# The third pass of a vision-state-space and attention kernel: square root and reciprocal in place of a power on GpSimd, one bias addition moved from VectorE to GpSimd, new planned durations

## The chip, the cores and the metric

The kernel runs on one core of a Trainium2 chip. The metric is the device time of one execution in microseconds (us), given as the median of several runs. A profile is one further execution with the hardware profiler on; it has its own time and its own span, from the first to the last recorded instruction. The engines are called TensorE (PE, and PEld for its weight loads), VectorE (DVE), ScalarE (ACT), GpSimd (POOL) and SyncE (SP), whose queue issues nearly all DMAs.

## The reference

The input x is 8 images of 64 x 64 positions with 96 channels. Two layers are computed.

Layer 0 normalises x in groups of three channels, projects it to 2 x 192 channels, runs a 3 x 3 depthwise convolution and then a selective scan in four directions over the 4096 positions of each image. Its end is what matters here: the sum y of the scans is standardised over its 192 channels, scaled and shifted, gated by silu(z), projected back to 96 channels and added to x.

```
mu = jnp.mean(y, axis=-1, keepdims=True)
var = jnp.mean(jnp.square(y - mu), axis=-1, keepdims=True)
y = (y - mu) * jax.lax.rsqrt(var + 1e-05) * ln_gamma + ln_beta
y = y * jax.nn.silu(z)
out = jnp.einsum('bhwd,cd->bhwc', y, out_proj_w)
```

Layer 1 is attention without a softmax over the tokens of an image, followed by a feed-forward part in quantised numbers (products in fp8, sums rounded to 16 bits). Each of the two stands behind a standardisation over the 96 channels, `(v - m) / sqrt(s + 1e-5)`, and is added to its input:

```
t = t + attn(_ln_t(t))
t = t + ffn(_ln_t(t))
```

Without a softmax, attention needs only the 97 x 97 Gram matrix of the standardised tokens of an image. So an image's tokens must all be standardised before the first of them can go on.

## The kernel before

There are three passes: projections and convolution; the scan; and everything behind the scan. The change lies in the third, `pass3`. It works on units of 512 tokens, held as 128 partitions x 4 blocks: 8 images x 8 units, 64 units in all.

Each unit goes through a load (five DMAs: the two halves y and yo of the scan's sum, two parts of the gate zs, and x as xr) and two generators.

- `first_part` (line 979): GpSimd adds y and yo; `standardize` on y; TensorE transposes y in two steps, ScalarE evicts each (gt) and GpSimd multiplies it by zs; TensorE projects; VectorE adds xr and so makes t; `standardize` on t, into ln; TensorE adds ln to the image's Gram matrix (pg) and transposes it, and ScalarE evicts that (lnT).
- `attention` (line 1031), once per image when its eight Gram contributions are in, makes a matrix weff from the Gram matrix by four small products.
- `second_part` (line 1058): TensorE multiplies lnT by weff, VectorE adds to t; `standardize` on t, into lf; transpose and cast to fp8 (xq, VectorE); three products with the first weights (ph), evicted to f16 by ScalarE twice and VectorE once (h); VectorE adds the first bias and takes the maximum with zero, three times; GpSimd casts to fp8 (hq); TensorE makes the second product (mm); ScalarE evicts it as f16 (y16, shown by the profile as `y<-mm`); VectorE adds the second bias b2q to it (`y<-y,b2q`); GpSimd adds it to t; SyncE stores t.

`standardize` (line 947) runs three times per unit, 192 times in all. VectorE makes statistics and aggregates of the four blocks; GpSimd adds 1e-5 to the four variances of each partition and raises them to the power -1/2 (the constant tile `mhalf`); VectorE multiplies mean and deviation; ScalarE applies scale and bias to the four blocks. The profile calls the small tile mvy, mvt or mvf by what it standardises: y, t, or t again for the feed-forward part.

The order of the instructions on each engine is written at build time by a planner, `weave` (line 142). A generator yields, ahead of each step, the engine's name, a duration that the planner assumes, and, if it differs from 0.3, a delay until the result can be used; a fourth value is a pool of buffers that the step takes from. The planner simulates five engines with these durations and always issues the step that could begin first, with ties broken by rank. Up to five first parts, five second parts and one load are open at a time, and a first part ranks twelve units ahead. What comes out is a fixed order: `InOrder` (line 82) makes every instruction on TensorE, VectorE, ScalarE and GpSimd, and every DMA that SyncE issues in the pass, follow the one issued before it on that engine. It records all of them at line 91, so the profile shows line 91 for nearly everything and groups are told apart by tile names. On the chip the durations play no part any more: an engine whose next instruction isn't ready waits, with everything behind it.

The delay of 20 behind the last GpSimd step is such a planned number. It puts the store of a unit later in SyncE's queue, where a store that waits would hold up the loads behind it.

Of the kernel before, what the change touches and what calls it, by code (L numbers as in the profile page):

```python
# [33 lines left out]
F32 = mybir.dt.float32  # L34
# [3 lines left out]
AF = mybir.ActivationFunctionType  # L38
ALU = mybir.AluOpType
# [3 lines left out]
P = 128  # L43
NB, HH, WW, C = 8, 64, 64, 96
# [823 lines left out]
def pass3(ctx, tc, g, ident, mhalf, engines, y_d, z_d, out):  # L868
    nc = tc.nc
    pe, dve, act, pool = engines  # L870
    CA = C + 1
    sp = InOrder(tc, nc.sync)
    wp = ctx.enter_context(tc.tile_pool(name="p3w", bufs=1))
# [4 lines left out]
    NU = GRP // P  # L878
# [5 lines left out]
    gates = ctx.enter_context(tc.tile_pool(name="p3gates", bufs=3))  # L884
    held = ctx.enter_context(tc.tile_pool(name="p3held", bufs=HELD))
    banks = {"tr": 3, "mm": 2, "ph": 2}
    slots = {name: Slots(count) for name, count in {**banks, "loaded": LOADED, "held": HELD, "gates": 3}.items()}
    pools = {name: ctx.enter_context(tc.tile_pool(name=f"p3{name}", bufs=count, space=PSUM)) for name, count in banks.items()}
    ps_one = ctx.enter_context(tc.tile_pool(name="p3ps", bufs=1, space=PSUM))

# [28 lines left out]
    def load_quantized(shape, src, name):  # L922
        raw = one.tile([P, *shape[1:]], F32, name=f"{name}_raw", tag="raw")
        if shape[0] < P:
            nc.vector.memset(raw[shape[0] : P], 0.0)
        nc.sync.dma_start(raw[0 : shape[0]], src)
        q = wp.tile([P, *shape[1:]], F8, name=name)
        nc.vector.tensor_copy(q, raw, saturate=False)
        return q
# [6 lines left out]
    b2q = load_quantized([P, C], g["b2"].unsqueeze(0).to_broadcast([P, C]), "b2q")  # L936
# [4 lines left out]
    def take(name, shape):  # L941
        return pools[name].tile(shape, F32, name=name), slots[name].taken

    def tokens(src, q):
        return src[q * GRP : (q + 1) * GRP].rearrange("(n p) c -> p n c", p=P)

    def standardize(src, dst, name, cost):

        yield "dve", 4 * cost
        st = each.tile([P, NU, 6], F32, name=f"st{name}")  # L950
        mv = each.tile([P, NU, 2], F32, name=f"mv{name}")
        for i in range(NU):
            dve.bn_stats(st[:, i, :], src[:, i, :])
        for i in range(NU):
            dve.bn_aggr(mv[:, i, :], st[:, i, :])
        yield "pool", 1.3
        pool.tensor_scalar(mv[:, :, 1], mv[:, :, 1], 1e-5, None, ALU.add)
        pool.tensor_tensor(mv[:, :, 1], mv[:, :, 1], mhalf[:, 0:NU], ALU.pow)
        yield "dve", 0.15
        dve.scalar_tensor_tensor(mv[:, :, 0], mv[:, :, 0], -1.0, mv[:, :, 1], ALU.mult, ALU.mult)  # L960
        yield "act", 4 * cost
        for i in range(NU):
            act.activation(dst[:, i, 0 : src.shape[2]], src[:, i, :], AF.Identity, bias=mv[:, i, 0:1], scale=mv[:, i, 1:2])
# [15 lines left out]
    def first_part(b, q):  # L979
        yield "load", b, q  # L980
        y, yo, zs, xr, of_loads = loads[b, q]
        yield "pool", 1.8, 0.3, slots["held"]
        t, lnT = held.tile([P, NU, C], F32, name="t"), held.tile([P, GRP], F32, name="lnT")
        holds[b, q] = t, lnT, slots["held"].taken
        pool.tensor_add(y, y, yo)
        yield from standardize(y, y, "y", 0.45)
        for i, ch in enumerate((slice(0, P), slice(DI - P, DI))):
            yield "pe", 0.6, 0.3, slots["tr"]
            pt, slot = take("tr", [P, GRP])
            for n in range(NU):  # L990
                pe.transpose(pt[:, n * P : (n + 1) * P], y[:, n, ch], ident)
            end = yield ("act", 0.65) if i else ("act", 0.65, 0.3, slots["gates"])
            if i == 0:
                gt, of_gt = gates.tile([P, 2, GRP], F32, name="gt"), slots["gates"].taken
            act.activation(gt[:, i, :], pt, AF.Identity, bias=gb[:, i, 1:2], scale=gb[:, i, 0:1])
            slots["tr"].release(slot, end)
            yield "pool", 1.3
            pool.tensor_mul(gt[:, i, :], gt[:, i, :], zs[:, i, :])
        end = yield "pe", 3.8, 0.3, slots["mm"]
        slots["gates"].release(of_gt, end)  # L1000
        po, slot = take("mm", [P, NU, C])
        for i in range(NU):
            blk = slice(i * P, (i + 1) * P)
            pe.matmul(po[:, i, :], gt[:, 0, blk], w_out0, start=True, stop=False)
            pe.matmul(po[:, i, :], gt[:, 1, blk], w_out1, start=False, stop=True)
        end = yield "dve", 0.55, 0.0
        dve.tensor_add(t, po, xr)
        slots["mm"].release(slot, end)
        slots["loaded"].release(of_loads, end)
        ln = lns[(b * UNITS + q) % OPEN]  # L1010
        yield from standardize(t, ln, "t", 0.35)
        if b > 0:
            yield "gram", b - 1
        end = yield "pe", 1.6
        if b not in grams:
            grams[b] = ps_one.tile([P, CA], F32, name="pg")
        counts["gram", b] = counts.get(("gram", b), 0) + 1
        for i in range(NU):
            first, last = counts["gram", b] == 1 and i == 0, counts["gram", b] == UNITS and i == NU - 1
            pe.matmul(grams[b], ln[:, i, :], ln[:, i, 0:CA], start=first, stop=last)  # L1020
        if counts["gram", b] == UNITS:
            done["grams", b] = end
        yield "pe", 0.7, 0.3, slots["tr"]
        pl, slot = take("tr", [P, GRP])
        for i in range(NU):
            pe.transpose(pl[:, i * P : (i + 1) * P], ln[:, i, :], ident)
        end = yield "act", 0.6
        act.copy(lnT, pl)
        slots["tr"].release(slot, end)
# [28 lines left out]
    def second_part(b, q):  # L1058
        yield "weff", b
        t, lnT, of_hold = holds[b, q]  # L1060
        end = yield "pe", 1.3, 0.3, slots["mm"]
        pa, slot = take("mm", [P, NU, C])
        for i in range(NU):
            blk = slice(i * P, (i + 1) * P)
            pe.matmul(pa[:, i, :], lnT[:, blk], weffs[b], start=True, stop=True)
        end = yield "dve", 0.55, 0.0
        dve.tensor_add(t, t, pa)
        slots["mm"].release(slot, end)
        lf = lfs[(b * UNITS + q) % OPEN]
        yield from standardize(t, lf, "f", 0.35)  # L1070

        yield "pe", 0.7, 0.3, slots["tr"]
        pf, slot = take("tr", [P, GRP])
        for i in range(NU):
            pe.transpose(pf[:, i * P : (i + 1) * P], lf[:, i, :], ident)
        end = yield "dve", 0.7
        xq = each.tile([P, GRP], F8, name="xq")
        dve.tensor_copy(xq, pf, saturate=False)
        slots["tr"].release(slot, end)
        h1 = each.tile([P, NHC, GRP], F16, name="h1")  # L1080
        for hc in range(NHC):
            yield "pe", 0.4, 0.3, slots["ph"]
            ph, slot = take("ph", [P, GRP])
            pe.matmul(ph, w1q[:, hc * P : (hc + 1) * P], xq, start=True, stop=True)
            end = yield ("act" if hc < 2 else "dve"), 0.6
            (act.copy if hc < 2 else dve.tensor_copy)(h1[:, hc, :], ph)
            slots["ph"].release(slot, end)
        yield "dve", 1.2
        for hc in range(NHC):
            dve.tensor_scalar(h1[:, hc, :], h1[:, hc, :], b1q[:, hc : hc + 1], 0.0, ALU.add, ALU.max)  # L1090
        yield "pool", 1.5
        hq = each.tile([P, NHC, GRP], F8, name="hq")
        pool.tensor_copy(hq, h1, saturate=False)
        yield "pe", 1.0, 0.3, slots["mm"]
        po, slot = take("mm", [P, NU, C])
        for i in range(NU):
            for hc in range(NHC):
                pe.matmul(po[:, i, :], hq[:, hc, i * P : (i + 1) * P], w2q[:, hc, :], start=hc == 0, stop=hc == NHC - 1)
        end = yield "act", 0.5
        y16 = each.tile([P, NU, C], F16, name="y16")  # L1100
        act.copy(y16, po)
        slots["mm"].release(slot, end)
        yield "dve", 0.6
        dve.tensor_add(y16, y16, b2q.unsqueeze(1).to_broadcast([P, NU, C]))

        yield "pool", 0.95, 20.0
        pool.tensor_add(t, t, y16)
        end = yield "sp", 0.7, 4.0
        sp.dma_start(tokens(out[b], q), t)
        slots["held"].release(of_hold, end)  # L1110
# [53 lines left out]
```

## Time and profile before

| | |
|---|---|
| median of 3 runs | 10,178.76 us (10,177.76 to 10,182.01) |
| the profiled execution's own time | 10,170.3 us |
| its span | 10,168.5 us |
| mean granted TensorE clock | 0.906 |
| busy over the whole span | TensorE 74%, VectorE 94%, ScalarE 90%, GpSimd 90% |
| third pass, from its first load to the last instruction | 9,328 to 10,169 us |
| busy in the third pass | TensorE 605.9 us, VectorE 635.8, ScalarE 523.2, GpSimd 672.6 |

Busy shares over the span say little on the third pass, since the scan takes most of the time and loads the engines otherwise. A row of a table of stages gives the stretch, its length, the busy time of each engine with its number of instructions, the granted TensorE clock, the mean busy share of the DMA engines and what they moved. A row of a group gives engine and operation, output and inputs by name, sizes and number; behind the first bar the busy time in us and the mean of one in ns, behind the second the idle time of the engine ahead of these instructions and what ended it. A row of the timeline gives start and duration in us, then the group, and in brackets the idle time ahead of it. A row of the waits gives who waited for whom: total us, times, longest.

### The profile page before, as it was taken

The numbers are of one execution on the slowest core, as the hardware profiler recorded it, in microseconds if no ns is written. First come the engines' busy times: TensorE is split into PE (matmuls) and PEld (weight loads), VectorE is DVE, ScalarE is ACT, GpSimd is POOL, SyncE is SP. The second block draws the span as 40 slices with busy tenths as digits, with TensorE's granted clock in tenths as the row PEclk, the third lists the DMA queues.
The fourth block names the chain that finished last, engine by engine and source line by source line (L and its number), as shares of the span: only waits on it lengthen the run. The fifth ranks groups of instructions, "written<-read, shape, count | busy, mean of one in ns | idle before, by whom it ended". The sixth has DMA issues, their size and how long they took to land.

```text
span 10168.5 us, 152388 instructions
## 1 busy us (share of the span) xinstructions
PE 7540.2 (74%) x52384; PEld 6239.7 (61%) x52384; DVE 9577.5 (94%) x6896; ACT 9175.2 (90%) x20499; POOL 9189.8 (90%) x3231
## 2 busy tenths in 40 slices
PE   7767777777777777777777777777777777776777
PEld 3336666665666666665666666666666666665665
DVE  7979999999999999999999999999999999997887
ACT  5669999999999999999999999999999999996665
POOL 1549999999999999999999999999999999997886
PEclk8889999989998999989989989899999999898887
DMA  5766776689976766799866666899666668997542
GB/s 164 236 213 219 228 232 220 228 209 208 208 221 212 227 219 214 226 205 202 224 209 223 221 212 224 209 207 208 218 215 224 217 214 222 206 204 191 156 140 72
DMA packets 932228, 2111.66 MB, mean 208 GB/s; under 512 B 274603, under 2 KB 422860, under 8 KB 929922
## 3 DMA queue, kind: packets, MB, share of 16 engines
q1 hardware_dynamic: 928650, 2100.57, 72.8%
q8 instruction: 419, 6.86, 0.3%
q14 instruction: 351, 2.88, 0.1%
q0 software_dynamic: 432, 0.94, 0.0%
q10 hardware_dynamic: 2376, 0.40, 0.0%
HBM read 1925.98 MB, written 175.66 MB: 207 GB/s over the span
## 4 chain that ended last, share of the span: by engine, by line
ACT 29%; DVE 28%; issue 16%; POOL 12%; PE 11%; DMA 3%; SPq 1%; DVEq 0%; ACTq 0%; POOLq 0%
DVE h L91 20%; ACT x L91 11%; ACT da L91 11%; POOL c L91 7%; PE acc L91 6%; DVE wide L91 5%; ACT L91 2%; PE wide L91 2%; ACT y L91 1%; POOL xg L91 1%; PE px L91 1%; ACT delta L91 1%; PE pa L91 1%; DMA xd_d<-xd 1%; DVE u L91 1%
## 5 line engine op out<-in xcount | busy, mean ns | idle before, releaser
L91 POOL TENSOR_TENSOR c<-c,h 128x2048 f32<-128x2048 f32 x1536 | 6957.3, 4553 | 292.5 <-issue 135.5
L91 DVE TENSOR_TENSOR_SCAN h<-da,carry,wide 128x1024 f32<-128x1024 f32 x2304 | 5267.8, 2331 | 133.6 <-PE wide L91 34.3
L91 ACT ACTIVATE x<-duT,bT 128x128 f32<-128x128 f32 (+1 forms) x13312 | 3994.9, 371 | 2.0
L91 PE MATMUL acc<-ident,c 128*128 128x128 f32 x24576 | 3429.8, 297 | 588.5 <-POOL c L91 581.1
L91 ACT ACTIVATE da<-delta,a_neg 128x1024 f32<-128x1024 f32 x3072 | 3520.6, 1147 | 290.4 <-DVE h L91 278.7
L91 PEld LDWEIGHTS acc<-ident,c 128*128 128x128 f32 x24576 | 3111.6, 154 | 1028.5 <-POOL c L91 918.8
L91 PE MATMUL wide<-ident,x 128*128 128x128 f32 x10752 | 1566.1, 291 | 636.5 <-DVE h L91 570.2
L91 PEld LDWEIGHTS wide<-ident,x 128*128 128x128 f32 x10752 | 1314.3, 150 | 831.0 <-ACT x L91 376.7
L91 DVE TENSOR_TENSOR_SCAN h<-da,wide 128x1024 f32<-128x1024 f32 x768 | 1712.4, 2271 | 43.9 <-PE wide L91 10.6
L91 DVE TENSOR_TENSOR wide<-du,wide 128x1024 f32<-128x1024 f32 x1280 | 1543.0, 1207 | 41.3 <-PE wide L91 40.9
L91 PE MATMUL wide<-xb,sel 96*128 96x512 bf16 x2560 | 819.8, 404 | 687.7 <-DVE h L91 671.0
L91 POOL TENSOR_TENSOR xg<-duT,bT 128x512 f32<-128x512 f32 (+1 forms) x640 | 892.4, 1409 | 27.5 <-PE wide L91 10.9
L91 PEld LDWEIGHTS <-sel 96*128 96x128 bf16 x2560 | 232.3, 102 | 867.2 <-DVE h L91 615.2
L91 PE MATMUL wide<-ident,xg 128*128 128x128 f32 x3584 | 481.1, 278 | 118.3 <-DVE h L91 116.3
L91 PEld LDWEIGHTS wide<-ident,xg 128*128 128x128 f32 x3584 | 409.6, 143 | 148.6 <-issue 110.6
L91 ACT ACT_TABLE_LOAD x385 | 494.0, 1283 | 6.8
L91 POOL TENSOR_TENSOR du<-delta,u 128x1024 f32<-128x1024 f32 x192 | 456.9, 2380 | 8.2 <-ACT delta L91 8.2
L91 DVE SCALAR_TENSOR_TENSOR u<-xpad,conv_w,u 128x4096 f32<-128x4096 f32 x96 | 452.0, 4708 | 1.9
L91 PE MATMUL px<-u,w_xp 128*128 128x512 f32 x512 | 250.2, 628 | 56.5 <-ACT u L91 41.8
L91 ACT COPY y<-acc 128x1024 f32<-128x1024 f32 x192 | 192.7, 1004 | 82.1 <-PE acc L91 81.8
L91 POOL TENSOR_TENSOR bq<-bq,bs 128x512 f32<-128x512 f32 (+1 forms) x48 | 117.7, 2453 | 162.7 <-ACT bs L91 116.3
L91 PE MATMUL wide<-ident,du 128*128 128x128 f32 x1536 | 206.9, 278 | 67.6 <-DVE h L91 34.3
(141 smaller groups left out, 6149.3 us busy)
## 6 DMA issues: line engine op xcount, KB each, us to landing
c<-xd_d SPq DMA_DIRECT2D x1024, 1024.0 KB
c<-xd_d SPq DMA_DIRECT2D x1024, 512.0 KB
u<-u_d SPq DMA_DIRECT2D x127, 512.0 KB
xdt<-dt_d SPq DMA_DIRECT2D x1146, 36.0 KB
xb<-b_d SPq DMA_DIRECT2D x382, 96.0 KB
u<-u_d SPq DMA_DIRECT2D x128, 256.0 KB
zs<-z_d SPq DMA_DIRECT2D x128, 256.0 KB
y_d<-y SPq DMA_DIRECT2D x24, 1024.0 KB
```

Source lines behind the costliest of these rows:

```text
L91: ins = getattr(self.engine, op)(*args, **kwargs).ins
```

## The change

The third pass gets a constant tile `eps` of 1e-5. In `standardize` the two GpSimd instructions go. ScalarE takes the square root of variance + eps instead (one instruction for the four variances), and VectorE makes the reciprocal in a further instruction, ahead of the product that was there. In `second_part` the addition of the second bias goes from VectorE to GpSimd, directly ahead of GpSimd's addition to t. The remaining edits are durations that the planner assumes: for the statistics and normalisations, the gate's evictions, the first bias, and the joined GpSimd step at the end.

```diff
+    eps = wp.tile([P, 1], F32, name="eps")
+    nc.vector.memset(eps, 1e-5)
...
     def standardize(src, dst, name, cost):
-        yield "dve", 4 * cost
+        yield "dve", 4 * (cost - 0.05)
...
-        yield "pool", 1.3
-        pool.tensor_scalar(mv[:, :, 1], mv[:, :, 1], 1e-5, None, ALU.add)
-        pool.tensor_tensor(mv[:, :, 1], mv[:, :, 1], mhalf[:, 0:NU], ALU.pow)
-        yield "dve", 0.15
+        yield "act", 0.25
+        act.activation(mv[:, :, 1], mv[:, :, 1], AF.Sqrt, bias=eps)
+        yield "dve", 0.4
+        dve.reciprocal(mv[:, :, 1], mv[:, :, 1])
         dve.scalar_tensor_tensor(mv[:, :, 0], mv[:, :, 0], -1.0, mv[:, :, 1], ALU.mult, ALU.mult)
         yield "act", 4 * cost
...
-        yield from standardize(y, y, "y", 0.45)
+        yield from standardize(y, y, "y", 0.54)
...
-            end = yield ("act", 0.65) if i else ("act", 0.65, 0.3, slots["gates"])
+            end = yield ("act", 0.77) if i else ("act", 0.77, 0.3, slots["gates"])
...
-        yield from standardize(t, ln, "t", 0.35)
+        yield from standardize(t, ln, "t", 0.46)
...
-        yield from standardize(t, lf, "f", 0.35)
+        yield from standardize(t, lf, "f", 0.46)
...
-        yield "dve", 1.2
+        yield "dve", 1.5
         for hc in range(NHC):
             dve.tensor_scalar(h1[:, hc, :], h1[:, hc, :], b1q[:, hc : hc + 1], 0.0, ALU.add, ALU.max)
...
-        yield "dve", 0.6
-        dve.tensor_add(y16, y16, b2q.unsqueeze(1).to_broadcast([P, NU, C]))
-        yield "pool", 0.95, 20.0
+        yield "pool", 2.2, 20.0
+        pool.tensor_add(y16, y16, b2q.unsqueeze(1).to_broadcast([P, NU, C]))
         pool.tensor_add(t, t, y16)
```

## The prediction

> **What bounds the kernel now.** Everything the change touches lies in the third pass, so I read the busy time by stage first: start-up; first parts alone (7 additions of the two scan halves); first and second parts mixed (52 such additions, 47 casts of the hidden layer); drain.
>
> ```profile
> core 0: us, PE busy (x) PEld busy (x) DVE busy (x) ACT busy (x) POOL busy (x), PEclk, DMA share, GB/s
> 9328.00:9374.00 46.00, 18.47 (x74) 14.61 (x74) 17.64 (x70) 13.68 (x27) 24.37 (x37) 0.53 0.86 249
> 9374.00:9434.00 60.00, 43.04 (x250) 39.40 (x250) 39.45 (x134) 36.57 (x78) 47.30 (x51) 0.77 0.58 177
> 9434.00:10035.00 601.00, 458.28 (x3245) 394.81 (x3246) 496.00 (x1807) 410.68 (x909) 530.50 (x557) 0.87 0.48 142
> 10035.00:10169.00 134.00, 86.10 (x529) 63.44 (x528) 82.69 (x295) 62.23 (x141) 70.48 (x77) 0.68 0.10 26
> ```
>
> The pass takes 841 of 10,168.5 us; a gain can come from nowhere else. In its main stage GpSimd is the fullest engine (530.5/601 = 88%), VectorE next (83%), ScalarE has 190 us free. The groups of this stretch say what fills GpSimd:
>
> ```profile
> L91 POOL TENSOR_TENSOR gt<-gt,zs 128x512 f32<-128x512 f32 x128 | 163.8, 1287 | 18.2 <-ACT gt L91 17.6 <-PE tr L91 0.4
> ...
> L91 POOL TENSOR_TENSOR mvt<-mvt,mhalf 128x4 f32<-128x4 f32 x64 | 67.5, 1055 | 5.3
> L91 POOL TENSOR_TENSOR mvf<-mvf,mhalf 128x4 f32<-128x4 f32 x64 | 67.4, 1053 | 5.3
> L91 POOL TENSOR_TENSOR mvy<-mvy,mhalf 128x4 f32<-128x4 f32 x64 | 66.5, 1040 | 5.3
> L91 POOL TENSOR_TENSOR t<-t,y 128x384 f32<-128x384 f32 x64 | 58.9, 921 | 29.0 <-DVE y L91 24.4 <-DVE mvf L91 2.7 <-DVE mvt L91 0.9
> ...
> L91 DVE SCALAR_TENSOR_TENSOR mvt<-mvt 128x4 f32<-128x4 f32 x64 | 51.8, 810 | 22.4 <-POOL mvt L91 21.7
> ...
> L91 DVE SCALAR_TENSOR_TENSOR mvy<-mvy 128x4 f32<-128x4 f32 x64 | 49.2, 770 | 39.2 <-POOL mvy L91 39.2
> ...
> L91 DVE TENSOR_TENSOR y<-y,b2q 128x384 f16<-128x384 f16 x64 | 43.7, 683 | 26.7 <-ACT y L91 26.7
> ...
> L91 POOL TENSOR_SCALAR mvt<-mvt 128x4 f32<-128x4 f32 x64 | 16.5, 258 | 34.2 <-DVE mvt L91 33.5 <-DVE mvy L91 0.3
> ```
>
> Four numbers to the power -1/2 take as long as 384 additions. And VectorE's product of the same four numbers takes 0.74 us on average (141.3 us over 192, mvf's 40.3 included), though its shortest took 0.126. The timeline of the second stage shows why:
>
> ```profile
> 9394.08 1.04 POOL L91 TENSOR_TENSOR mvy<-mvy,mhalf 128x4 f32<-128x4 f32 x1
> 9395.09 1.81 POOL L91 TENSOR_TENSOR y<-y,yo 128x768 f32<-128x768 f32 x1
> 9395.16 1.77 DVE L91 SCALAR_TENSOR_TENSOR mvy<-mvy 128x4 f32<-128x4 f32 x1 [2.56 <-POOL mvy L91]
> ...
> 9397.02 1.87 ACT L91 ACTIVATE y<-y,mvy 128x192 f32<-128x192 f32 x4 [2.83 <-DVE mvy L91]
> ```
>
> The power ends, GpSimd goes straight to its next addition, and VectorE's product, released at the same moment, ends with that addition. ScalarE waits for both. Here this closes a loop of 8.53 us per unit: two gate products (2.49), add and power (1.3), blocked product (1.8), normalisation (1.9), transpose and eviction (1.1). Who waited, in the main stage:
>
> ```profile
> ACT lf L91 <- DVE mvf L91: 53.6, 33, 4.5
> ACT ln L91 <- DVE mvt L91: 39.0, 27, 4.5
> ACT y L91 <- DVE mvy L91: 37.3, 21, 4.5
> ```
>
> **What the Trainium skill says.** "SBUF — State Buffer", section "Who interferes with whom": a VectorE instruction with two SBUF inputs, and casts, copies and tensor_scalar in two-port modes, are shut out while a GpSimd instruction that reads SBUF runs. The trace agrees (0.126 us free, 1.77 behind the addition). "ScalarE: Activation LUTs", section "Table sets: the hidden batching unit": copy and identity are in every set, so the square root's set serves the whole pass. The built order confirms it: one more table load than before, ahead of the first square root, none after; 1.28 us by the trace's 494.0/385.
>
> **The change part by part** (main stage: 153 standardisations, about 46 bias additions).
>
> 1. GpSimd loses 153 adds and powers: 160.4 us of powers (all instructions that read the -1/2 constants in this stage) + 153 x 0.249 = 198.5 us.
> 2. GpSimd gains 46 bias additions, f16 plus fp8, 384 elements. Not in this trace on GpSimd. Below: 0.83 us, the 2.6 cycles per element of "GPSIMD Engine Reference", section "3.1 Elementwise — side-by-side cycle accounting", an estimate; the 0.921 row is close. Above: the third-way-split subtractions of the first pass, mean 2.45 us for 512 elements, so 1.84. I take 1.1: 51 us. GpSimd: 530.5 - 198.5 + 51 = 383 (417 at the upper end, still not the fullest).
> 3. ScalarE gains 153 square roots of four numbers. Its copy of two numbers takes 0.178 us; the ScalarE page (section "What ACT_TABLE_LOAD costs") gives 280 ns + 0.833 per element with a pointer bias, an estimate of 0.283. I take 0.28: 43 us, 410.7 to 454. Its 190 free us hide this; without that cover it costs the 43.
> 4. VectorE loses 46 x 0.683 = 31 us and gains 153 reciprocals. No row; the shortest four-number product (0.126) is the floor, a reciprocal shut out as those products are (0.74) the ceiling. I take 0.16, as a one-input instruction on strided numbers: 24 us.
> 5. The products and bias-and-ReLU steps are shut out less, as GpSimd falls from 88% to about 70% full and no longer starts an operation at the product's release. Product: 0.155 free + 0.7 x 0.65 (half a mean GpSimd operation) = 0.6 for 0.74, 21 us. ReLU: three take 0.86 us where they run free in the timeline, 0.29 each, so 141 x (0.549 - 0.29) = 36 us lost today, a quarter less: 9. VectorE: 496 - 31 + 24 - 30 = 459.
> 6. New waits. The square root stands on ScalarE's queue until VectorE's aggregates are done; behind it are normalisations, evictions and hidden-layer casts of other units, for which TensorE's banks wait. The reciprocal holds VectorE until ScalarE is done; behind it are the casts to fp8 and the ReLU, for which TensorE and GpSimd's cast wait. These replace the same two hand-offs through GpSimd. The bias addition no longer heads VectorE's queue (26.7 us idle before it).
> 7. The plan's costs change only the order. In the built order the first second part follows 12 first parts instead of 11, and 12 second parts run alone at the end as before; every queue up to this pass keeps its order. DMAs are the same ones in slightly another order; at 48% DMA share I cost that at nothing, and at 5 us if loads come late.
>
> Main stage: the fullest engine becomes VectorE (459; ScalarE 454, TensorE 458 with modelled ends). GpSimd reached 88% of the stage; with three engines level I take 85%: 459/0.85 = 540, gain 61. Second stage: the loop opens, ScalarE's work per first part is 1.87 + 1.55 + 1.55 + 0.57 + 0.56 = 6.1 us; with hand-offs 7.1 for 8.5, 7 units: gain 10. Start-up, bound by loads (86% DMA share): 0. Drain, a chain of latencies: power and blocked product save about 0.8 us per link, the slower addition gives back 0.5: gain 3. Sum 74 us. The profiled execution took 10,170.3 us (span and 1.8 around it), 8.5 under the median, so 10,170.3 - 74 + 8.5 = 10,105.
>
> **The rivals.**
> - Stronger: the engines were held mostly by blocked products. Main stage at 92%: 459/0.92 = 499, gain 102; second stage at ScalarE's 6.1, gain 17; drain 13. 10,047. For: 130 us of ScalarE waiting in the lines above. Against: nothing here runs at 92%.
> - Weaker: the wait moves to square roots heading ScalarE's queue. Main stage at 80%: 574, gain 27, others 5: 10,147. For: ScalarE in program order is now on both sides of each standardisation.
> - No change: these waits eat all 74. 10,179.
> - Slower: the reciprocal is shut out by GpSimd as well. A pair of reciprocal and product at 1.5 us: VectorE 496 - 31 - 153 x 0.74 + 153 x 1.5 = 581; at 90% full 646, 45 lost: 10,224. It decides from about 1.2 us per pair, where VectorE's sum reaches today's 530. Against: one input, and the skill's section doesn't name it.
> - That each square root reloads tables is excluded by the built order.
>
> **How the numbers follow.** Likeliest 0.58 (own range 10,075 to 10,135), stronger 0.17, weaker 0.16, no change 0.05, slower 0.04. A measurement tells from no change about 0.2%, 20 us. The weaker case lies partly inside: faster 0.58 + 0.17 + 0.12 = 0.87; same 0.09; slower 0.04. The range 10,040 to 10,160 leaves out the last two cases, a tail of the stronger one and a little of the weaker.
>
> **What would show it.** Right: powers gone, GpSimd near 70% of a main stage of about 540 us, products at 0.6 us or less, reciprocals near 0.16, bias additions near 1.1, the second stage's period near 7 us, one table load. Wrong: reciprocals or products near 0.7 and VectorE above 90%; ScalarE idle ahead of square roots for over 100 us; a drain longer than 140 us.

## The result, and the profile after

The changed kernel takes 10,116.26 us (median of 4 runs, 10,114.86 to 10,131.87) against 10,178.26 before (median of 4): a ratio of 0.9941 (95% interval 0.9928 to 0.9953), 62 us faster. The forecast was 10,105, 74 us faster. The direction came out as forecast and the size near it. Of the steps behind them the prices and the opened loop of the second stage held; three steps of the sum did not (part 5, the rule for the main stage, part 7).

The profiled execution happens to be the longest of the four. The difference lies ahead of the change: its third pass began at 9,346.7 us, that of the kernel before at 9,328.1, though both issue the same instructions until there. Such scatter of the first two passes goes through all profiled executions of this study (9,328 to 9,347 us). So beside each median I give the third pass alone, from its first load of `yo` to the last instruction of the profiled execution: 840.4 us before, 783.4 after, 57 less. It is one execution each, so a few us of it may be chance.

The busy time by stage after, with the same four stages as in the prediction:

```profile
core 0: us, PE busy (x) PEld busy (x) DVE busy (x) ACT busy (x) POOL busy (x), PEclk, DMA share, GB/s
9347.00:9393.00 46.00, 18.94 (x93) 15.88 (x94) 16.85 (x80) 18.75 (x40) 20.81 (x28) 0.60 0.88 254
9393.00:9435.00 42.00, 33.06 (x232) 29.73 (x232) 31.27 (x146) 36.59 (x87) 26.75 (x20) 0.92 0.78 240
9435.00:10003.00 568.00, 442.88 (x3225) 386.86 (x3226) 482.07 (x1913) 439.69 (x1067) 374.07 (x298) 0.87 0.50 150
10003.00:10130.00 127.00, 87.41 (x549) 65.18 (x547) 78.69 (x297) 63.82 (x154) 59.96 (x55) 0.67 0.10 27
```

The main stage ends here with the last normalisation of y. Cut in the same way, the kernel before has 607 us of main stage and 128 of drain:

```profile
9434.00:10041.00 607.00, 461.43 (x3261) 396.40 (x3262) 501.85 (x1831) 415.88 (x921) 535.06 (x562) 0.86 0.47 141
```

So the gain is 18 us in the second stage (60 to 42, for the same 7 additions), 39 in the main stage, 1 in the drain. GpSimd's share of the main stage falls from 88% to 66%.

The groups after, over the third pass, that answer to those of the prediction:

```profile
L91 POOL TENSOR_TENSOR gt<-gt,zs 128x512 f32<-128x512 f32 x128 | 161.8, 1275 | 132.1 <-ACT gt L91 111.9 <-DMA zs<-z_d 15.1 <-PE tr L91 3.4
...
L91 POOL TENSOR_TENSOR t<-t,y 128x384 f32<-128x384 f32 x64 | 58.4, 912 | 5.0
...
L91 POOL TENSOR_TENSOR y<-y,b2q 128x384 f16<-128x384 f16 x64 | 56.0, 875 | 52.1 <-ACT y L91 52.0
...
L91 DVE SCALAR_TENSOR_TENSOR mvt<-mvt 128x4 f32<-128x4 f32 x64 | 46.6, 729 | 2.2
...
L91 DVE SCALAR_TENSOR_TENSOR mvy<-mvy 128x4 f32<-128x4 f32 x64 | 41.2, 643 | 2.2
...
L91 ACT ACTIVATE mvt<-mvt,eps 128x4 f32<-128x4 f32 x64 | 19.1, 298 | 15.4 <-DVE mvt L91 14.9 <-DVE mvy L91 0.3
...
L91 DVE RECIPROCAL mvt<-mvt 128x4 f32<-128x4 f32 x64 | 10.8, 168 | 10.1 <-ACT mvt L91 9.9
```

The square root takes 0.298 us, the reciprocal 0.168, the bias addition on GpSimd 0.875. The product of mean and deviation is still long: with mvf's 38.9 us, 126.7 over 192, 0.66 us. The timeline shows both sides of that, shortly before the second stage begins:

```profile
9384.53 0.18 DVE L91 RECIPROCAL mvy<-mvy 128x4 f32<-128x4 f32 x1 [3.33 <-ACT mvy L91]
9384.75 0.26 DVE L91 SCALAR_TENSOR_TENSOR mvy<-mvy 128x4 f32<-128x4 f32 x1
...
9391.54 1.81 POOL L91 TENSOR_TENSOR y<-y,yo 128x768 f32<-128x768 f32 x1
...
9391.73 1.65 DVE L91 SCALAR_TENSOR_TENSOR mvy<-mvy 128x4 f32<-128x4 f32 x1
```

The first product runs nearly free. The second meets GpSimd's addition and ends with it, as before the change. In the second stage before, 13 of the 14 products met a GpSimd addition or product from its start, since GpSimd began it at the product's release; their mean there fell from 1.42 us to 0.82. With that the loop opened: 42/7 = 6.0 us per unit for 8.5. In the main stage nearly as much is held up as before (0.70 us per product before, 0.67 after).

The waits in the main stage after, total us, times and longest:

```profile
ACT ln L91 <- DVE mvt L91: 30.9, 21, 3.8
...
ACT lf L91 <- DVE mvf L91: 20.7, 14, 3.4
...
ACT mvt L91 <- DVE mvt L91: 11.7, 9, 3.9
ACT mvf L91 <- DVE mvf L91: 11.6, 11, 2.5
ACT y L91 <- DVE mvy L91: 11.3, 10, 2.1
...
ACT mvy L91 <- DVE mvy L91: 9.8, 6, 4.5
```

In the main stage ScalarE waited 130 us for VectorE's products; it now waits 63 for them and 33 for the aggregates, ahead of the square roots.

### The profile page after: what moved, and what is told of

Its sections match the earlier page's. It is cut to its first block, busy times and chain, and to the rows that moved or that the text cites. A ratio compares the mean times of both kernels' runs of the same rounds, so it can differ in the third digit from the quotient of the medians.

```text
span 10130.1 us, 152413 instructions
## 1 busy us (share of the span) xinstructions
PE 7527.0 (74%) x52384; PEld 6235.5 (62%) x52384; DVE 9551.4 (94%) x7025; ACT 9186.9 (91%) x20692; POOL 8990.2 (89%) x2911
## 4 chain that ended last, share of the span: by engine, by line
DVE 30%; ACT 29%; issue 15%; PE 13%; POOL 9%; DMA 3%; SPq 1%; DVEq 0%; ACTq 0%; POOLq 0%
DVE h L91 20%; ACT x L91 11%; ACT da L91 10%; POOL c L91 7%; PE acc L91 6%; DVE wide L91 5%; PE wide L91 3%; ACT L91 2%; ACT y L91 1%; POOL xg L91 1%; PE px L91 1%; PE pa L91 1%; ACT delta L91 1%; DMA xd_d<-xd 1%; DVE u L91 1%
## 5 line engine op out<-in xcount | busy, mean ns | idle before, releaser
L91 POOL TENSOR_TENSOR gt<-gt,zs 128x512 f32<-128x512 f32 x128 | 161.8, 1275 | 132.1 <-ACT gt L91 111.9
```

Source lines behind the costliest of these rows:

```text
L91: ins = getattr(self.engine, op)(*args, **kwargs).ins
```

## The experiments

Every experiment edits only the third pass. Differences to the changed kernel are given as medians, then as third pass. The kernel before took between 10,164 and 10,195 us in its 34 runs of one session, and each third pass is one execution; so a few us between two kernels are not told from none.

| kernel | median us | ratio to before, 95% interval | third pass us |
|---|---|---|---|
| before | 10,178 to 10,181 | | 840.4 |
| changed | 10,116.3 | 0.9941 (0.9928 to 0.9953) | 783.4 |
| power_only | 10,118.0 | 0.9939 (0.9927 to 0.9952) | 779.2 |
| bias_only | 10,201.4 | 1.0022 (1.0015 to 1.0029) | 862.6 |
| durations_only | 10,164.1 | 0.9985 (0.9978 to 0.9992) | 824.1 |
| old_durations | 10,135.6 | 0.9957 (0.9940 to 0.9973) | 798.1 |
| more_scalar | 10,122.8 | 0.9942 (0.9926 to 0.9959) | 783.8 |
| more_vector | 10,114.6 | 0.9938 (0.9923 to 0.9952) | 779.7 |
| more_gpsimd | 10,145.5 | 0.9968 (0.9956 to 0.9980) | 801.5 |
| open_four | 10,154.2 | 0.9975 (0.9964 to 0.9985) | 816.1 |
| open_six | 10,098.9 | 0.9918 (0.9904 to 0.9933) | 764.4 |
| product_on_gpsimd | 10,094.5 | 0.9915 (0.9901 to 0.9928) | 754.4 |
| product_gpsimd_bias_vector | 10,091.0 | 0.9910 (0.9895 to 0.9925) | 747.2 |
| product_bias_six | 10,087.9 | 0.9905 (0.9888 to 0.9921) | 744.8 |

**The parts of the change, one by one.** First the changed kernel with the bias addition back on VectorE:

```diff
-        yield "pool", 2.2, 20.0
-        pool.tensor_add(y16, y16, b2q.unsqueeze(1).to_broadcast([P, NU, C]))
+        yield "dve", 0.6
+        dve.tensor_add(y16, y16, b2q.unsqueeze(1).to_broadcast([P, NU, C]))
+        yield "pool", 0.95, 20.0
```

> The changed kernel with the second bias put back on VectorE; the power is still replaced and the new planned durations stay. Theory 1 (the fullest engine of the main stage sets its length): VectorE gets back about 48 x 0.68 = 33 us in the main stage, 482 + 33 = 515 at 85% full is 605 us, as long as before the change; only the second stage's 18 us stay. So about 20 us faster than before (10,158), and the bias move is worth about 40. Theory 2 (the power's trip through GpSimd was the whole matter): the bias move is worth nothing, 55 to 65 us faster than before.

61 us faster than before: as fast as the whole change. Theory 1 falls on its own number. The stage table of this kernel:

```profile
9427.00:9992.00 565.00, 442.68 (x3261) 390.99 (x3262) 501.17 (x1981) 441.50 (x1075) 336.62 (x251) 0.87 0.51 151
```

VectorE has 501 us, as much as before the change, in 565 us of main stage: 89% full, and the stage is no longer than with VectorE at 85%. Its busy time doesn't set the length.

The other two parts, each alone in the kernel before (the diff just shown the other way round; and the planned durations of the change for the steps that both kernels have, without any new instruction):

> The kernel before with only the second bias moved to GpSimd. Theory 1: GpSimd's main stage grows from 535 by 48 x 0.88 = 42 us to 577, at 88% full 656 us: 40 to 50 us slower than before (10,225). Theory 2 (what matters is the wait at the head of VectorE's queue that goes): 10 to 25 us faster than before.

> The kernel before with only the new planned durations of the steps that both kernels have: every instruction is the same, the order differs. Theory 1: the order is worth little, between 10 us faster and 10 slower than before. Theory 3 (the gain came from the order): 30 us or more faster.

The bias move alone costs 22 us, in the direction of theory 1 and at half its size. The durations alone bring 15 us, more than theory 1 allowed. Their counterpart sets them back in the changed kernel:

```diff
-        yield "dve", 4 * (cost - 0.05)
+        yield "dve", 4 * cost
...
-        yield from standardize(y, y, "y", 0.54)
+        yield from standardize(y, y, "y", 0.45)
...
-        yield "dve", 1.5
+        yield "dve", 1.2
```

(and likewise the two other standardisations to 0.35 and the gate's evictions to 0.65).

> The changed kernel with the planned durations of the steps that both kernels have set back to the old ones; the instructions stay changed. So far the durations alone brought 15 us and the replaced power with them 61. If the order's share adds up with the rest, this kernel is about 15 us slower than the changed one (third pass 799 us for 783). If the new durations only mattered together with the power on GpSimd, or only chance orders differ, within 6 us of it.

19 us slower than the changed kernel, 15 by the third pass. The order is worth some 15 us in either company, so about a quarter of the gain; the new instructions are worth the rest. Since the bias move adds nothing clear beside the replaced power, that rest, some 45 us, is put down to the power's replacement; the power replaced alone, under the old durations, was not run. The second stage speaks for the same split: it still takes 61 us in durations_only, and 42 in power_only as in the changed kernel.

**What an engine's time is worth.** Three kernels add work that nothing waits for: a second square root behind each square root; two reciprocals behind each product; three powers per unit behind steps of GpSimd's own. Spare is a small tile of ones. The planned duration of each of these steps is raised by what is added, and its delay is shortened by as much; the order may still differ from that of the changed kernel, which by itself can be worth some 15 us. The diffs leave out the tile and these durations.

```diff
         act.activation(mv[:, :, 1], mv[:, :, 1], AF.Sqrt, bias=eps)
+        act.activation(spare[:, :, 1], spare[:, :, 1], AF.Sqrt, bias=eps)
```

> The changed kernel with a second square root of four spare numbers behind each of the 192: 192 x 0.30 = 57 us more on ScalarE, of which some 43 in the main stage (440 to 483 of 568). Theory 1 (VectorE is the fullest engine): less than half of it shows, under 28 us slower than the changed kernel. Rival (square roots at the head of ScalarE's queue set the pace): 45 us or more.

```diff
         dve.scalar_tensor_tensor(mv[:, :, 0], mv[:, :, 0], -1.0, mv[:, :, 1], ALU.mult, ALU.mult)
+        dve.reciprocal(spare[:, :, 1], spare[:, :, 1])
+        dve.reciprocal(spare[:, :, 1], spare[:, :, 1])
```

> The changed kernel with two more reciprocals of four spare numbers behind each product: 384 x 0.165 = 63 us more on VectorE, some 50 in the main stage (482 to 532). Theory 1: it shows in full, 45 to 70 us slower than the changed kernel. Rival: under 30 us.

```diff
         pool.tensor_add(y, y, yo)
+        pool.tensor_tensor(spare[:, :, 1], spare[:, :, 1], mhalf[:, 0:NU], ALU.pow)
...
             pool.tensor_mul(gt[:, i, :], gt[:, i, :], zs[:, i, :])
+            if i:
+                pool.tensor_tensor(spare[:, :, 1], spare[:, :, 1], mhalf[:, 0:NU], ALU.pow)
...
         pool.tensor_copy(hq, h1, saturate=False)
+        pool.tensor_tensor(spare[:, :, 1], spare[:, :, 1], mhalf[:, 0:NU], ALU.pow)
```

> The changed kernel with three more powers of four spare numbers per unit on GpSimd, each behind one of its own steps: 192 x 1.04 = 200 us more, some 155 in the main stage (374 to 529 of 568, as full as before the change). What is put on GpSimd waits for nothing and nothing waits for it. If GpSimd's occupancy alone was what cost time before, the gain of the change goes: 40 us or more slower than the changed kernel. If the power cost through its place in the chain of each standardisation, under 20 us. Besides: if the power doesn't shut VectorE out while it runs, VectorE's products stay at 0.66 us and the ReLU steps at 0.56; if every GpSimd instruction does, they grow by a third.

ScalarE's 56 us cost 6 by the medians and nothing by the third pass; VectorE's 66 us cost nothing (2 and 4 us less). This contradicts theory 1, which wanted 45 us or more for VectorE's. VectorE's busy time in the pass rose by 33 us only, from 609 to 642: its other instructions took less by the remaining half. The groups of more_vector and of more_gpsimd, third pass:

```profile
L91 DVE RECIPROCAL spare<-spare 128x4 f32<-128x4 f32 x384 | 66.4, 173 | 6.5
```

```profile
L91 POOL TENSOR_TENSOR spare<-spare,mhalf 128x4 f32<-128x4 f32 x192 | 196.2, 1022 | 0.0
...
L91 DVE SCALAR_TENSOR_TENSOR mvt<-mvt 128x4 f32<-128x4 f32 x64 | 39.2, 613 | 2.2
...
L91 DVE SCALAR_TENSOR_TENSOR mvf<-mvf 128x4 f32<-128x4 f32 x64 | 33.3, 521 | 2.2
...
L91 DVE SCALAR_TENSOR_TENSOR mvy<-mvy 128x4 f32<-128x4 f32 x64 | 27.5, 430 | 2.2
```

196 us of powers off the chain cost 29 us by the medians, 18 by the third pass; neither reading reaches the 40 of an occupancy cause, and one lies above the 20 of the other. So part of the gain was GpSimd's time: roughly two fifths to two thirds of the 45 us, if the order's scatter is left aside. The rest is left for the power's place in the chain. Whether that is the shorter trip itself, or that GpSimd no longer starts a long step at the product's release, was not separated.

VectorE's products became shorter beside 196 us of powers, 0.52 us instead of 0.66; the bias-and-ReLU steps went from 0.56 to 0.59, far from a third more. So the power doesn't shut VectorE out. In this trace 58 of the 192 products ran wholly within a power, each in 0.16 to 0.17 us, as here:

```profile
9711.01 1.01 POOL L91 TENSOR_TENSOR spare<-spare,mhalf 128x4 f32<-128x4 f32 x1
...
9711.23 0.17 DVE L91 SCALAR_TENSOR_TENSOR mvf<-mvf 128x4 f32<-128x4 f32 x1
```

The timeline of the kernel before, in its drain, had shown it for the other kind:

```profile
10147.29 1.04 POOL L91 TENSOR_TENSOR mvf<-mvf,mhalf 128x4 f32<-128x4 f32 x1
10147.39 0.86 DVE L91 TENSOR_SCALAR h<-h,b1q 128x512 f16<-128x512 f16 x3
```

Three bias-and-ReLU steps run at their shortest, all inside one power.

**Latency over the number of open units.**

```diff
-    OPEN = 5
+    OPEN = 4
```

> The changed kernel with four first and four second parts open at a time in place of five. Adding 57 us of work to ScalarE or 66 us to VectorE cost nothing, so no engine's occupancy sets the pace. Theory 5 (the latency of a unit over the number of open units sets it): the third pass, fill and drain of some 170 us aside, takes up to 5/4 as long: 60 to 150 us slower than the changed kernel. Rival (occupancy and shut-out time of the engines together): under 30 us.

```diff
-    OPEN = 5
+    OPEN = 6
...
-    LOADED, HELD = 5, 20
+    LOADED, HELD = 5, 17
```

> The changed kernel with six of each open, and 17 buffers in place of 20 for what is held between first and second part, since memory allows no more. Theory 5: 25 us or more faster than the changed kernel, unless the fewer held buffers bind. Rival: within 10 us.

38 us slower (33 by the third pass) and 17 us faster (19). Neither theory's number holds: a pace set by latency alone would have cost 60 or more, one set by the engines alone would have left open_six within 10. The number of open units matters, partly. As orders alone move 15 us, these kernels have other orders too, and open_six has three held buffers less, I take no finer size from them.

**Taking the product off VectorE.** The sign and the product become two instructions on GpSimd:

```diff
-        yield "dve", 0.4
+        yield "dve", 0.2
         dve.reciprocal(mv[:, :, 1], mv[:, :, 1])
-        dve.scalar_tensor_tensor(mv[:, :, 0], mv[:, :, 0], -1.0, mv[:, :, 1], ALU.mult, ALU.mult)
+        yield "pool", 0.7
+        pool.tensor_scalar(mv[:, :, 0], mv[:, :, 0], -1.0, None, ALU.mult)
+        pool.tensor_tensor(mv[:, :, 0], mv[:, :, 0], mv[:, :, 1], ALU.mult)
```

> The changed kernel with the product of mean and deviation moved from VectorE to GpSimd, where it takes two instructions (a sign and a product, about 0.25 and 0.35 us). Theory 1 (VectorE is the fullest engine, and its products are shut out by GpSimd): VectorE's main stage falls from 482 by 150 x 0.66 to 383 us, GpSimd rises from 374 to 464, ScalarE 440, TensorE 443; at 85% full 546 for 568: 20 us faster than the changed kernel (10,096). Theory 4 (the chain of hand-offs per standardisation sets the pace): one more hand-off on a queue in order, 10 us or more slower than the changed kernel.

22 us faster than the changed kernel, 29 by the third pass, in spite of one more hand-off: theory 4 falls. Its groups and its main stage:

```profile
L91 POOL TENSOR_SCALAR mvt<-mvt 128x4 f32<-128x4 f32 x64 | 14.4, 226 | 4.8 <-DVE mvt L91 4.7
...
L91 POOL TENSOR_TENSOR mvt<-mvt 128x4 f32<-128x4 f32 x64 | 12.8, 200 | 15.9 <-DVE mvt L91 7.6 <-DVE mvy L91 2.2 <-DMA zs<-z_d 1.7
```

```profile
9425.00:9972.00 547.00, 442.43 (x3307) 381.15 (x3307) 395.39 (x1800) 445.71 (x1088) 440.85 (x617) 0.89 0.54 157
```

0.43 us on GpSimd, where the sign took 0.21 to 0.32 and the product 0.20 to 0.21, replaces 0.66 on VectorE that spread from 0.16 to 1.77. VectorE falls to 395 us of 547. The stage came out at the forecast 546 or so, but not for theory 1's reason, since in more_vector more work on VectorE cost nothing. What fits both is the length and spread of the products in the chain and at the head of VectorE's queue; that is argued, not shown.

Two more put things together:

> The product on GpSimd, as in product_on_gpsimd, and the second bias back on VectorE. VectorE is rid of the blocked products (127 us in the pass) and has room for the bias addition (46 us); GpSimd loses 56 us, of instructions that shut VectorE out. If shut-out time is what is left: 10 to 25 us faster than product_on_gpsimd (10,075). If VectorE's addition at the head of its queue costs as much: the same as product_on_gpsimd.

> Product on GpSimd, second bias on VectorE, six first and second parts open, 17 held buffers. If the two gains are of different kinds (shut-out time, and latency over the number of open units) they add: third pass 747 - 19 = 728 us, 10,072 in all. If both only shorten the same waits: within 8 us of the third pass's 747.

The first (the two diffs of power_only and product_on_gpsimd joined) is 7 us faster in the third pass than product_on_gpsimd and 3.5 by the medians, less than the 10 that shut-out time would have brought and not clear of the scatter. The second (with the diff of open_six as well) has the lowest median of the study, 10,087.9 us, 28 below the changed one; but against the first it gains 2 us in the third pass, where six open units brought 19 to the changed kernel. The expectation called this case one of shortening the same waits; which waits these are, no run shows.

## Why the prediction was right, and where its sum was not

The time lies in the range and 12 us from the forecast, with a gain of 62 us for 74. By its steps:

- Parts 1 to 4, the prices, held: GpSimd's main stage 374 us (383 forecast), bias addition 0.875 (1.1, near the lower bound), square root 0.298 (0.28), reciprocal 0.165 and at most 0.181 (0.16, never shut out, so the slower rival had no ground), one table load of 1.28 us.
- Second stage: the loop opened as forecast; 18 us gained for 10. At 6.0 us per unit it came to what only the stronger rival had taken, the 6.1 of ScalarE's own work.
- Part 5 failed. It took GpSimd's falling share as falling shut-out time, 30 us on VectorE. In the main stage the product went from 0.70 to 0.67 us (0.6 forecast) and the bias-and-ReLU step from 0.59 to 0.63 (lines below). The share that went was the powers', which held nothing up; the additions, products and casts that do were all still there, with one addition more per unit. In the third pass 136 of the 192 products took more than 0.17 us after the change, 106 before, and every one of them ended within 0.03 us of the end of a GpSimd addition, product or cast, none with a power. The rule that the prediction took from the Trainium skill, by which the product is shut out beside any GpSimd instruction that reads SBUF, doesn't hold for the power here; the measurement decides. The trace before could have told: a product of 0.126 us, the length that the prediction took as free, ran at 9,803.40 inside a power (9,803.19 to 9,804.23).
- The main stage's rule, the fullest engine over 0.85, failed as a rule. VectorE was at 85% (482/568), but at 89% in power_only with the same length, and took 66 us more for nothing in more_vector. Busy time of an instruction that is shut out is waiting, so a sum of busy times is no measure of the work. The bias move, 31 us off VectorE in part 4, was worth nothing clear beside the replaced power (2 us by the medians, 4 the other way by the third pass). The stage gained 39 us for 61 and took 568 us, not some 540.
- Part 7 put the new order at nothing. It brought 15 us.
- Drain: 1 us for 3. There was little shut-out time to save: 13 of the 17 products of the drain before ran in 0.17 us or less.

The bias-and-ReLU steps of the main stage, before and after:

```profile
L91 DVE TENSOR_SCALAR h<-h,b1q 128x512 f16<-128x512 f16 x144 | 77.4, 591 | 0.0
...
L91 DVE TENSOR_SCALAR h<-h,b1q 128x512 f16<-128x512 f16 x141 | 80.5, 625 | 0.0
```

Some readings in the prediction were loose too. The means of 0.549, 0.74 and 0.683 us in parts 4 and 5 are those of the whole pass (0.59, 0.70 and 0.72 in the main stage); the 0.29 of a free bias-and-ReLU step is a third of three that overlap, while each by itself lasts 0.34; the shortest product took 0.121, not 0.126.

That the total came near is luck in part: without the order's 15 us, which wasn't in it, the forecast would have been 27 us off. Open is what sets the pace of the third pass after the change. More work on VectorE or ScalarE lengthened it by nothing clear; GpSimd's time, the number of open units and the place of the product each moved it in part, and the last two didn't add.

## What to carry to other kernels

A small instruction between two engines in a chain can cost more than the time it takes of its engine. Replacing a power of 1.04 us by two instructions of 0.30 and 0.17 on other engines brought some 45 us, about 60 with the new durations, while 196 us of the same powers off the chain cost only 18 to 29. Before a gain is put down to a relieved engine, see which of its instructions really hold the other one up, and don't count time in which an instruction is shut out as work. Where the order is written from assumed durations, new durations are a change of their own and are to be measured alone.

## What the runs showed of the hardware

GpSimd's power on four numbers per partition (1.04 us) left VectorE free: bias-and-ReLU steps ran at their shortest within it, and 58 two-input products that ran within one took 0.16 to 0.17 us each. Its additions, products and casts did hold such products up: all 136 longer ones after the change ended with one. VectorE's reciprocal of four numbers was never held up (at most 0.18 us). GpSimd's product of four numbers took 0.20 us and its sign change 0.23; VectorE's single product of the same four, 0.66 on average beside GpSimd's larger operations. GpSimd's addition of f16 and fp8 with a broadcast operand (384 elements) took 0.875 us, no longer than f32 plus f16 at 0.912.
